# A graph attention layer in float32: Strassen's block products for the weights, and (A h) W for A (h W)

## The chip, the core and the metric

The kernel runs on one core of a Trainium2 chip. The core has a matmul engine (TensorE, PE in the profile; PEld is its weight load), three engines for elementwise work (VectorE: DVE, ScalarE: ACT, GpSimd: POOL), and SyncE (SP), which here only issues transfers between the chip's memory and the core's. TensorE reads operands from SBUF and writes to PSUM, which has eight banks of 512 float32 values in each of 128 partitions. Each engine works through its own list of instructions in order, and semaphores tie the lists together. The metric is the device time of one execution in microseconds (us).

## The reference

The input x has 128 batches of 64 nodes with 512 features, one adjacency matrix serves all batches, and everything is float32:

```
h   = relu(layernorm(x))
Wh  = h W[head]                       # four heads, 512 -> 512
e   = leaky_relu(f1[n] + f2[m], 0.01) # f1, f2: Wh times the halves of a
A   = softmax(e where adj > 0 else -1e9)
h1  = elu(concat over heads of A Wh)  # 2048 features
Wh2 = h1 W_out                        # 2048 -> 512, one head, the same attention
o   = elu(A2 Wh2)
y   = relu(o w1 + b1) w2 + b2 + o
out = x + layernorm(y) * gamma + beta
```

The weights are ten matrices of 512 x 512: four of W, four of W_out, w1 and w2. The product of a tile of 128 tokens with all of them is 10 x 16 matmuls of 128 x 128 with 128 x 512.

## The kernel before

Two batches share a tile of 128 tokens, which gives 64 tiles; inside a tile the attention matrix is block-diagonal, with zeros between the two batches. All weights lie in SBUF from the start on (wh, wo, w1s, w2s). The main loop takes a tile through stages that are staggered over three tiles, so that the vector work of one lies under the matmuls of another:

- `norm1` (L91 to L97): mean and variance on VectorE (L83, L85), the power -0.5 on GpSimd (L89), relu with scale and bias on ScalarE (hn).
- `transpose_h`, `project1`: four transposes, f1 and f2 of all heads (pf, L238) and then, for each head, h W in four matmuls of 512 columns (pm, L244), which ScalarE copies out (L248).
- `softmax` on VectorE and ScalarE; the scores come from one matmul (pe, L182).
- `attend1`: A (h W), transposed: for each head four matmuls of 128 columns (pa, L258), then elu (L227 to L229).
- `project2`: 16 matmuls of 512 columns (pm, L276), and f of the second layer from the result (jf, L284).
- `attend2`, `transpose_out`, and after every fourth tile `feed_forward` on the group of four (L314, L322) with the last layer norm (L326 to L329) and the store.

SyncE issues the loads of x and of adj and the stores of the output; the weights and rows were loaded on ScalarE's queue, the rows of a_heads on GpSimd's. The tile framework sets the order: each engine's list comes from a scheduler that plans the whole program with its own estimates of time, so instructions of different stages interleave in the list, and buffers that are reused bring waits.

A float32 matmul is two instructions on TensorE in the profile (2048 rows for the 1024 matmuls of L244); a transpose is one.

Of the kernel before, what the change touches and what calls it, by code (L numbers as in the profile page):

```python
# [15 lines left out]
NEG = 1.0e9  # L16
# [4 lines left out]
def gat_preln_kernel(  # L21
# [16 lines left out]
    """x + GAT(relu(LN(x))): two batches of 64 nodes share one tile of 128 tokens; attention inside  # L38
    a tile is block-diagonal. Feed-forward runs on groups of G tiles. Everything is float32."""
# [9 lines left out]
    OC = O // P  # L49
    FC = FO // P  # L50
    DC = DF // P
    NT = B * N // P
    G = 4

# [9 lines left out]
    def row_bcast(dst, src):  # L64
        """A row of DRAM into all partitions."""
        nc.scalar.dma_start(out=dst, in_=src[None, :].to_broadcast([P, src.shape[0]]))

# [1 line left out]
    X, HN, HT = {}, {}, {}  # L69

    def load(t):
        X[t] = xp.tile([P, F], FP, tag="x", name=f"x{t}")
        nc.sync.dma_start(out=X[t], in_=xf[ts(t, P), :])
# [5 lines left out]

    def norm_stats(src, tag, t):  # L80
        """mean and (var + eps)^-0.5 per token."""
# [10 lines left out]
    def norm1(t):  # L92
        mean, rstd = norm_stats(X[t], "n1", t)
        nb = sm.tile([P, 1], FP, tag="n1nb", name=f"n1nb{t}")
        nc.vector.scalar_tensor_tensor(nb, mean, -1.0, rstd, ALU.mult, ALU.mult)
        HN[t] = wk.tile([P, F], FP, tag="hn", name=f"hn{t}")
        nc.scalar.activation(HN[t], X[t], AF.Relu, bias=nb, scale=rstd)  # L97

    def transpose_h(t):
        pt = ps.tile([P, KC, P], FP, tag="tp", name=f"pth{t}")  # L100
        for k in range(KC):
            nc.tensor.transpose(pt[:, k, :], HN[t][:, ts(k, P)], ident)
        HT[t] = wk.tile([P, KC, P], FP, tag="hT", name=f"hT{t}")
        nc.scalar.copy(HT[t], pt)  # L104
        del HN[t]

    load(0)

# [1 line left out]
    wh = const.tile([P, H, KC, O], FP, name="wh")  # L110
    for h in range(H):
        nc.scalar.dma_start(out=wh[:, h], in_=W_heads[h].rearrange("(k p) o -> p k o", p=P))
    load(1)
    load(2)
    norm1(0)

    aj = const.tile([P, N], mybir.dt.int32, name="aj")
    for b in range(NB):
        nc.sync.dma_start(out=aj[ts(b, N), :], in_=adj)
    adjm = const.tile([P, N], FP, name="adjm")  # L120
    nc.vector.tensor_scalar(adjm, aj, 0.0, None, ALU.is_gt)
    negm = const.tile([P, N], FP, name="negm")
    nc.vector.tensor_scalar(negm, adjm, NEG, -NEG, ALU.mult, ALU.add)

    blkones = const.tile([P, NB, N], FP, name="blkones")
    nc.vector.memset(blkones, 0.0)
    for b in range(NB):
        nc.vector.memset(blkones[ts(b, N), b, :], 1.0)
    eye = const.tile([P, N], FP, name="eye")
    nc.vector.tensor_add(eye, ident[:, 0:N], ident[:, N:2 * N])  # L130

    # f1 and f2 of the heads are h @ (W a): wa[k, (c, h)] = sum_o W[h, k, o] a[h, c, o].
    wa = const.tile([P, KC, 2 * H], FP, name="wa")
    for c in range(2):
        for h in range(H):
            ab = wk.tile([P, O], FP, tag="y", name=f"ab{c}_{h}")
            nc.gpsimd.dma_start(
                out=ab, in_=a_heads[h:h + 1, c * O:(c + 1) * O].to_broadcast([P, O])
            )
            for k in range(KC):  # L140
                junk = wk.tile([P, FO], FP, tag="junk", name=f"jk{c}_{h}_{k}", bufs=1)
                nc.vector.scalar_tensor_tensor(  # L142
                    junk, wh[:, h, k, :], 1.0, ab, ALU.mult, ALU.mult,
                    accum_out=wa[:, k, c * H + h:c * H + h + 1],
                )

    wo = const.tile([P, H * OC, FO], FP, name="wo")
    for h in range(H):
        nc.scalar.dma_start(
            out=wo[:, ts(h, OC), :],  # L150
            in_=W_out[h * O:(h + 1) * O, :].rearrange("(c p) o -> p c o", p=P),
        )
    ao = const.tile([P, 2, FO], FP, name="ao")
    for c in range(2):
        row_bcast(ao[:, c, :], a_out[c * FO:(c + 1) * FO])
    w1s = const.tile([P, FC, DF], FP, name="w1s")
    nc.scalar.dma_start(out=w1s, in_=w1.rearrange("(k p) d -> p k d", p=P))
    b1s = const.tile([P, DC], FP, name="b1s")
    for d in range(DC):
        nc.scalar.dma_start(out=b1s[:, d:d + 1], in_=b1[ts(d, P)][:, None])  # L160
    w2s = const.tile([P, DC, FO], FP, name="w2s")
    nc.scalar.dma_start(out=w2s, in_=w2.rearrange("(k p) d -> p k d", p=P))
    b2s = const.tile([P, FO], FP, name="b2s")
    row_bcast(b2s, b2)
# [169 lines left out]
    for i in range(NT + 2):  # L334
        if i + 3 < NT:
            load(i + 3)
# [49 lines left out]
```

## Time and profile before

| | |
|---|---|
| median of 3 runs | 2804.86 us (2804.45 to 2805.07) |
| span of the profiled execution, first to last instruction | 2802.2 us |
| its own time around the span, taken as the median less the span | 2.7 us |
| PE busy | 2708.3 us, 97% |
| DVE, ACT, POOL busy | 1185.1, 567.8, 263.5 us |
| moved by DMA | 48.98 MB, mean 17 GB/s |
| granted TensorE clock | 0.997 of full speed |

In the rows of groups a line reads: line of the code, engine, operation, tile written <- tiles read, shape, count, then busy time, mean duration of one in ns, and the idle time of the engine in front of them with what ended it. Rows of the timeline begin with the start and the duration in us. Matmuls are pipelined and their ends are modelled, so the time that one takes of PE is the distance between two starts, not its duration. The rows of windows give, for each stretch, its length and then the busy time with the count in brackets for PE, PEld, DVE, ACT and POOL, the granted clock, the DMA engines' busy share and GB/s.

### The profile page before, as it was taken

Reading aid. Unit: us, or ns where it says so; the run is one execution under the profiler, and the core shown is the slowest. Engines: PE = TensorE matmul, PEld = TensorE weight load, DVE = VectorE, ACT = ScalarE, POOL = GpSimd, SP = SyncE. Lnnn points to the kernel's source line nnn. Section 1 sums busy time; section 2 is a strip of 40 time slices with the busy share of each in tenths; the row PEclk is TensorE's granted clock in tenths of the full one; section 3 lists DMA queues with packets and bytes.
Section 4 is the critical chain, followed back from the end, with each engine's and each line's share of the span. In section 5 each row is a group of like instructions: output and inputs, shape, how many; then the busy total and the mean of one; then the engine's idle time right before and its main releaser. Section 6 shows DMA issues by size and latency. Waiting matters only on the chain.

```text
span 2802.2 us, 23483 instructions
## 1 busy us (share of the span) xinstructions
PE 2708.3 (97%) x8896; PEld 1407.5 (50%) x8896; DVE 1185.1 (42%) x3206; ACT 567.8 (20%) x1025; POOL 263.5 (9%) x271
## 2 busy tenths in 40 slices
PE   3999999999999999999999999999999999999997
PEld 1555555545455454554555555454554545545553
DVE  5344435444254443444444344443544435434433
ACT  1221221212212121121212212122121211212121
POOL 2001001010010101001011010100101000010000
PEclk9999999999999999999999999999999999999998
DMA  6000000000000000000000000000000000000000
GB/s 233 1 0 27 4 1 30 1 31 0 0 31 1 31 1 8 23 1 30 1 23 8 1 31 0 30 1 0 31 1 30 0 1 31 0 27 1 10 6 15
DMA packets 25920, 48.98 MB, mean 17 GB/s; under 512 B 3152, under 2 KB 3152, under 8 KB 25808
## 3 DMA queue, kind: packets, MB, share of 16 engines
q1 hardware_dynamic: 18592, 33.60, 3.6%
q10 hardware_dynamic: 6576, 11.80, 1.2%
q0 software_dynamic: 640, 2.10, 0.2%
q8 instruction: 69, 1.13, 0.2%
q14 instruction: 43, 0.35, 0.0%
HBM read 30.71 MB, written 16.78 MB: 17 GB/s over the span
## 4 chain that ended last, share of the span: by engine, by line
PE 86%; DVE 7%; ACT 2%; POOL 2%; issue 2%; DMA 1%; SPq 0%; POOLq 0%; DVEq 0%; ACTq 0%
PE pm L276 31%; PE pm L244 30%; PE pa L258 8%; PE pf L314 8%; PE pf L322 2%; PE pa L292 2%; POOL n2rs L89 2%; PE pf L238 1%; DVE y L326 1%; ACT wh L280 1%; DVE n2st L83 1%; PE s1pe L182 1%; DVE jf L284 1%; ACT outT L303 1%; DMA ab<-in_L_gnn_a_heads_dram 1%
## 5 line engine op out<-in xcount | busy, mean ns | idle before, releaser
L244 PE MATMUL pm<-wh,hT 128*128 128x512 f32 x2048 | 924.0, 598 | 0.3 <-ACT hT L104 0.3
L276 PE MATMUL pm<-wo,h1T 128*128 128x512 f32 x2048 | 900.1, 592 | 0.0
L276 PEld LDWEIGHTS pm<-wo,h1T 128*128 128x128 f32 x2048 | 384.1, 190 | 476.6 <-issue 476.6
L244 PEld LDWEIGHTS pm<-wh,hT 128*128 128x128 f32 x2048 | 378.6, 190 | 399.2 <-issue 392.1
L284 DVE SCALAR_TENSOR_TENSOR jf<-pm,ao 128x512 f32<-128x512 f32 x128 | 88.5, 691 | 757.4 <-ACT wh L280 755.3
L227 ACT ACTIVATE ex<-pa 128x512 f32<-128x512 f32 x320 | 190.7, 596 | 538.4 <-PE pa L258 458.4
L248 ACT COPY wh<-pm 128x512 f32<-128x512 f32 x256 | 150.0, 586 | 636.1 <-PE pm L244 629.8
L258 PEld LDWEIGHTS pa<-s1AT,wh 128*128 128x128 f32 x2048 | 244.2, 192 | 54.2 <-issue 27.1
L304 POOL TENSOR_TENSOR o<-o,b2s 128x512 f32<-128x512 f32 x64 | 81.5, 1273 | 1977.7 <-PE pto L302 1977.7
L258 PE MATMUL pa<-s1AT,wh 128*128 128x128 f32 x2048 | 254.1, 277 | 10.1 <-DVE s1AT L221 9.3
L314 PE MATMUL pf<-outT,w1s 128*128 128x512 f32 x512 | 230.1, 603 | 5.0 <-ACT outT L303 5.0
L322 PE MATMUL pf<-w2s,rT 128*128 128x512 f32 x512 | 222.3, 592 | 0.0
L228 DVE TENSOR_SCALAR ex<-ex 128x512 f32<-128x512 f32 x320 | 133.2, 420 | 201.0 <-ACT ex L227 200.0
L280 ACT COPY wh<-pm 128x512 f32<-128x512 f32 x64 | 37.5, 586 | 784.9 <-PE pm L276 784.9
L229 DVE SCALAR_TENSOR_TENSOR h1T<-pa,ex 128x512 f32<-128x512 f32 x256 | 173.9, 684 | 5.6
L322 PEld LDWEIGHTS pf<-w2s,rT 128*128 128x128 f32 x512 | 97.3, 190 | 122.5 <-issue 118.6
L314 PEld LDWEIGHTS pf<-outT,w1s 128*128 128x128 f32 x512 | 95.9, 192 | 118.3 <-issue 109.3
L221 DVE COPY s2AT<-s2pt 128x128 f32<-128x128 f32 x64 | 18.6, 291 | 286.2 <-PE s2pt L219 286.1
L326 DVE TENSOR_TENSOR y<-pf,o 128x512 f32<-128x512 f32 x64 | 43.6, 681 | 213.1 <-PE pf L322 213.1
L89 POOL TENSOR_TENSOR n2rs<-n2ve,mhalf 128x1 f32<-128x1 f32 x64 | 60.8, 951 | 394.6 <-DVE n2ve L87 394.6
L238 PE MATMUL pf<-wa,hT 128*128 128x8 f32 x512 | 62.7, 248 | 30.8 <-DVE jk L142 30.3
L305 POOL TENSOR_TENSOR x<-x,bs 128x512 f32<-128x512 f32 x64 | 81.5, 1273 | 21.1 <-ACT hn L97 17.9
(73 smaller groups left out, 1604.3 us busy)
## 6 DMA issues: line engine op xcount, KB each, us to landing
x<-in_x_dram SPq DMA_DIRECT2D x64, 256.0 KB, 2.7
out_dram<-y SPq DMA_DIRECT2D x64, 256.0 KB, 2.0
wh<-in_L_gnn_W_heads_dram ACTq DMA_DIRECT2D x4, 1024.0 KB, 9.7
wo<-in_L_gnn_W_out_dram ACTq DMA_DIRECT2D x4, 1024.0 KB, 15.6
ab<-in_L_gnn_a_heads_dram POOLq DMA_DIRECT2D x8, 256.0 KB, 5.8
w1s<-in_L_gnn_w_dram ACTq DMA_DIRECT2D x1, 1024.0 KB, 13.6
w2s<-in_L_gnn_w_dram ACTq DMA_DIRECT2D x1, 1024.0 KB, 7.6
ao<-in_L_gnn_a_out_dram ACTq DMA_DIRECT2D x2, 256.0 KB, 14.2
```

Of the source, the lines that this page charges most:

```text
L89: nc.gpsimd.tensor_tensor(rstd, ve, mhalf, ALU.pow)
L227: nc.scalar.activation(ex, src, AF.Exp)
L228: nc.vector.tensor_scalar(ex, ex, 1.0, -1.0, ALU.min, ALU.add)
L229: nc.vector.scalar_tensor_tensor(dst, src, 0.0, ex, ALU.max, ALU.add)
L238: nc.tensor.matmul(pf, hT[:, k, :], wa[:, k, :], start=(k == 0), stop=(k == KC - 1))
L244: nc.tensor.matmul(pm, hT[:, k, :], wh[:, h, k, :], start=(k == 0), stop=(k == KC - 1))
L248: nc.scalar.copy(WH1[t, h], pm)
L258: nc.tensor.matmul(pa[:, c, :], w[:, ts(c, P)], AT[:, h, :], start=True, stop=True)
L276: nc.tensor.matmul(pm, hT[:, c, :], wo[:, i, :], start=(i == 0), stop=(i == H * OC - 1))
L284: nc.vector.scalar_tensor_tensor(junk, pm, 1.0, ao[:, c, :], ALU.mult, ALU.mult, accum_out=f[:, c:c + 1])
L314: nc.tensor.matmul(pm, w1s[:, k, ts(d, P)], oT[:, k, :], start=(k == 0), stop=(k == FC - 1))
L322: nc.tensor.matmul(pm, rT[:, d, ts(j, P)], w2s[:, d, :], start=(d == 0), stop=(d == DC - 1))
```

## The change

The kernel is written anew around groups of four tiles (512 tokens), 16 of them. Three things change in what is computed.

**Products in seven block products.** A group's activations are cut into four blocks of 256 tokens by 256 features, a weight matrix into four blocks of 256 x 256, and the product is formed by Strassen's scheme in the variant of Winograd: seven products of 256 x 256 blocks instead of eight. The sums of weight blocks are made once at the start (`prepare`, on GpSimd) and stored in the chip's memory (tc); the sums of activations are made by GpSimd for layers 1 and 2 (`sums`, `each`) and by VectorE for the feed-forward (`blocks`). The results are combined partly in PSUM (p2, p7, p3 and p4 add into the bank of an earlier product) and partly by VectorE (t, s15, and the last sums).

**Weights streamed.** No weight matrix stays in SBUF. `piece` loads the 256 x 256 block or sum that a product needs, 256 KB, on SyncE's queue into a ring of 12 buffers: 70 pieces for a group, 1120 in all. 480 of them come from the weights themselves in rows of 1 KB, 640 from the stored sums in rows of 2 KB. x is loaded into two buffers and loaded again for the residual (xr).

**(A h) W in layer 1.** The attention is applied to h, in front of W. For each tile, half of the features and batch, two matmuls of 256 columns (all four heads) read 64 partitions, the first batch on the upper half of PE's rows and the second on the lower half, into two PSUM banks (L403). ScalarE and VectorE each copy one of them out (L413, L415). The elu becomes two passes on ScalarE and one on VectorE (L423 to L425).

The order of a group in the program: `project1` for four heads, `attend1` of the next group, `feed_forward` of the group before, `project2`; norms and softmaxes (`stage_a`, two groups ahead) and the second attention (`stage_e`) are given out in pieces between the products (`side`). The last product of a unit (`late`) runs after the first two of the next one.

```diff
-    xp = ctx.enter_context(tc.tile_pool(name="xp", bufs=9))
+    ring = ctx.enter_context(tc.tile_pool(name="ring", bufs=12))
+    big = ctx.enter_context(tc.tile_pool(name="big", bufs=1))
...
-    ps = ctx.enter_context(tc.tile_pool(name="ps", bufs=2, space=bass.MemoryType.PSUM))
+    dram = ctx.enter_context(tc.tile_pool(name="dram", bufs=1, space=bass.MemoryType.DRAM))
+    ps = ctx.enter_context(tc.tile_pool(name="ps", bufs=6, space=bass.MemoryType.PSUM))
...
+    def prepare(m):
+        w = big.tile([P, KC, O], FP, tag=("h11", "h12")[m % 2], name=f"pw{m}")
+        nc.scalar.dma_start(out=w, in_=mats[m].rearrange("(k p) o -> p k o", p=P))
...
+        s = big.tile([P, 4, 2, Q], FP, tag=("h22", "hS")[m % 2], name=f"pt{m}")
+        nc.gpsimd.tensor_tensor(s[:, 0], b12, b11, ALU.subtract)
+        nc.gpsimd.tensor_tensor(s[:, 2], b22, b12, ALU.subtract)
+        nc.gpsimd.tensor_tensor(s[:, 1], b22, s[:, 0], ALU.subtract)
+        nc.gpsimd.tensor_tensor(s[:, 3], b21, s[:, 1], ALU.subtract)
+        TC[m] = dram.tile([P, 4, 2, Q], FP, name=f"tc{m}")
+        nc.sync.dma_start(out=TC[m], in_=s)
+
+    def piece(m, p):
+        w = ring.tile([P, 2, Q], FP, tag="w", name=f"w{m}_{p}")
...
+        nc.sync.dma_start(out=w, in_=src)
+        return w
...
+        def p1():
+            gb[1] = bank(f"g1_{name}")
+            product(1, gb[1], True)
+            gb["s1"] = wk.tile([P, 2, T], FP, tag="s1", name=f"s1_{name}")
+            nc.scalar.copy(gb["s1"], gb[1])
+
+        def p6():
+            gb[6] = bank(f"g6_{name}")
+            product(6, gb[6], True)
+            gb["t"] = wk.tile([P, 2, T], FP, tag="t", name=f"t_{name}")
+            nc.vector.tensor_tensor(gb["t"], gb[6], gb["s1"], ALU.add)
+            post("t", gb["t"])
...
+        def p7():
+            product(7, gb[6], False)
+            post("c22", gb[6], gb["s15"])
...
+        return [p1, p6, p5, p2, p7, p3, p4]
...
+            for o in range(2):
+                for k in range(2):
+                    nc.tensor.matmul(
+                        bk[:, o, :], w[:, k, ts(o, P)], a[:, k, :],
+                        start=first and o == 0 and k == 0, stop=k == 1, skip_group_check=True,
+                    )
...
+    def sums(s1, a11, a12, a22, s2, s3, s4):
+        nc.gpsimd.tensor_tensor(s2, s1, a11, ALU.subtract)
+        nc.gpsimd.tensor_tensor(s4, a12, s2, ALU.subtract)
+        nc.gpsimd.tensor_tensor(s3, a22, s2, ALU.subtract)
...
+                for c in range(2):
+                    for b in range(NB):
+                        rows = slice(b * N, (b + 1) * N)
+                        nc.tensor.matmul(
+                            banks[b][:, c, :].rearrange("p (h n) -> p h n", h=H),
+                            src[rows, off + c * P:off + (c + 1) * P],
+                            at[rows, :, rows], start=True, stop=True, skip_group_check=True,
+                        )
...
+            s1, a22 = tt[1][:, 0:2], tt[1][:, 2:4]
+            nc.vector.tensor_tensor(s1, s1, a22, ALU.add)
+            nc.vector.tensor_tensor(s2, s1, a11, ALU.subtract)
...
+    for g in range(NG):
+        if g >= 1:
+            side.extend(stage_e(g - 1))
+        for h in range(H):
+            project1(g, h)
+        flush_side()
+        flush_late()
+        if g + 1 < NG:
+            attend1(g + 1)
+        if g >= 1:
+            feed_forward(g - 1)
+            flush_late()
+        side.extend(stage_a(g + 2))
+        project2(g)
+        flush_side()
```

How the lists move, at three places. First TensorE, where a tile's layer 1 stood and where (A h) of the next group now follows the last products of a head (before, then the change; pm and pa are products and attention, g a product's bank, w a piece, z and zs blocks of (A h) and their sums, pz a bank of (A h), at the attention, hn the tile):

```order
L244 MATMUL pm_7_0_1577<-wh,hT_1486 128x512 x2
L258 MATMUL pa_2_1550<-s1AT_1528,wh_6_2_1428 128x128 x4
L258 MATMUL pa_3_1560<-s1AT_1528,wh_6_3_1435 128x128 x4
L182 MATMUL s1pe_1586<-s1dg_1584,blkones 128x256
L244 MATMUL pm_7_1_1605<-wh,hT_1486 128x512 x4
```
```order
L229 MATMUL g_a_3_2843<-zs_z_3_2777,w_3_2873 128x256 x4
L229 MATMUL g_a_3_2822<-z_2_1846,w_4_2884 128x256 x4
L403 MATMUL pz_12_0_2900<-at_2469,hn_2265 128x256
L403 MATMUL pz_12_1_2901<-at_2469,hn_2265 128x256
L403 MATMUL pz_12_0_2900<-at_2469,hn_2265 128x256
L403 MATMUL pz_12_1_2901<-at_2469,hn_2265 128x256
```

The attention's short matmuls between the products are gone; a block product is one row of four matmuls of 256 columns, and (A h) stands as a phase of its own in which the two batches alternate.

Second VectorE: before, at the end of a group, among the last layer norms (y, n2); in the change at the end of (A h) and the start of the feed-forward (x, n1 are the first norm; ot the transposed output o; zs_o its sums). The semaphores that a row waits for stand behind it:

```order
L83 BN_STATS n1st_2549<-x_2170 128x6 [waits DMAHW7_49]
L326 TENSOR_TENSOR y_2139<-pf_6_2134,o_1820 128x512 [waits DMAHW6_49,PE_49]
L85 BN_AGGR n1mv_2551<-n1st_2549 128x2 [waits DVE_49]
L83 BN_STATS n2st_2141<-y_2139 128x6 [waits DVE_49]
L87 TENSOR_SCALAR n1ve_2553<-n1mv_2551 128x1 [waits DVE_49]
```
```order
L262 BN_STATS n1st_4361<-x_3443 128x6 [waits DMAHW3_49]
L415 COPY z_3_2899<-pz_15_1_2957 128x2x4x64 [waits PE_49]
L264 BN_AGGR n1mv_4363<-n1st_4361 128x2 [waits DVE_49]
L266 TENSOR_SCALAR n1ve_4365<-n1mv_4363 128x1 [waits DVE_49]
L276 SCALAR_TENSOR_TENSOR n1nb_4369<-n1mv_4363,n1rs_4367 128x1 [waits Activation_49,Pool_49]
L555 TENSOR_TENSOR ot_1_2965<-ot_1_2965 128x512 [waits Activation_49]
L262 BN_STATS n1st_4373<-x_3445 128x6 [waits DMAHW4_49]
L556 TENSOR_TENSOR zs_o_2996<-ot_1_2965,ot_1_2964 128x512 [waits DVE_49]
```

All four norms of a later group have moved into this phase, and L555 and L556, which make operands of the feed-forward's products, stand behind the loads of x.

Third SyncE, before in the middle of the program, in the change between the feed-forward's and layer 2's pieces (w a piece, tc a stored sum):

```order
L73 DMA x_6420<-in_x_dram 128x512 [waits DMAHW7_49,Pool_49]
L330 DMA out_dram<-y_6371 128x512 [waits DMAHW0_49,DVE_49]
L73 DMA x_6609<-in_x_dram 128x512 [waits DMAHW1_49,Pool_49]
L330 DMA out_dram<-y_6389 128x512 [waits DMAHW2_49,DVE_49]
L73 DMA x_6797<-in_x_dram 128x512 [waits DMAHW3_49,Pool_49]
```
```order
L151 DMA w_7_3113<-tc_445 128x512 [waits DMAHW0_49,PE_49]
L92 DMA x_3332<-in_x_dram 128x512 [waits DMAHW1_49,Activation_49]
L92 DMA x_3334<-in_x_dram 128x512 [waits DMAHW2_49,Activation_49]
L92 DMA x_3443<-in_x_dram 128x512 [waits DMAHW3_49,DMAHW1_49,Activation_49]
L92 DMA x_3445<-in_x_dram 128x512 [waits DMAHW4_49,DMAHW2_49,Activation_49]
L151 DMA w_3_3121<-in_L_gnn_w_dram 128x2x256 [waits DMAHW5_49,PE_49]
```

Loads of x and stores that had a queue to themselves now stand among the weight pieces.

More of the change, by code (lines that the diff above doesn't have):

```diff
@@ new lines, in gat_preln_kernel @@
+    blkones = const.tile([P, NB, N], FP, name="blkones")
+    nc.vector.memset(blkones, 0.0)
+    for b in range(NB):
+        nc.vector.memset(blkones[ts(b, N), b, :], 1.0)
+    eye = const.tile([P, N], FP, name="eye")
+    nc.vector.tensor_add(eye, ident[:, 0:N], ident[:, N:2 * N])
+    mats = [W_heads[h] for h in range(H)]
+    mats += [W_out[h * O:(h + 1) * O, :] for h in range(H)]
+    mats += [w1, w2]
+    M1, M2 = H * 2, H * 2 + 1
+    TC = {}
+    wa = const.tile([P, KC, 2 * H], FP, name="wa")
```

572 lines of the change are left out of this document (362 added, 210 removed).

## The prediction

> **What bounds the kernel now.** I read the page's busy times first, then the chain that ended last, then a steady stretch by windows, then single stretches of the timeline.
>
> ```profile
> PE 2708.3 (97%) x8896; PEld 1407.5 (50%) x8896; DVE 1185.1 (42%) x3206; ACT 567.8 (20%) x1025; POOL 263.5 (9%) x271
> PE 86%; DVE 7%; ACT 2%; POOL 2%; issue 2%; DMA 1%; SPq 0%; POOLq 0%; DVEq 0%; ACTq 0%
> ...
> 1457.32 0.99 POOL L89 TENSOR_TENSOR n2rs<-n2ve,mhalf 128x1 f32<-128x1 f32 x1 [17.11 <-DVE n2ve L87]
> 1627.92 0.99 POOL L89 TENSOR_TENSOR n2rs<-n2ve,mhalf 128x1 f32<-128x1 f32 x1 [17.11 <-DVE n2ve L87]
> 1457.30:1627.90 170.60, 168.70 (x557) 87.73 (x556) 72.28 (x197) 35.40 (x64) 16.07 (x16) 1.00 0.04 13
> ...
> 50.07 2.91 PE L244 MATMUL pm<-wh,hT 128*128 128x512 f32 x3
> ```
>
> The same norm of two successive groups of four tiles stands 170.60 us apart, and the window over one such period has PE busy for 168.70 of it, DVE for 72.28, POOL for 16.07 (its columns are PE, PEld, DVE, ACT, POOL). The kernel is TensorE's matmul stream. So I split the profiled span of 2802.2 us into a start of 50.1 (the first weight product), 16 periods of 170.6 (2729.6) and a rest of 22.5 at the end. The median of the runs is 2.7 above the span; I add that at the end.
>
> What a matmul instruction takes of PE is read from start to start, since the printed durations overlap:
>
> ```profile
> 1400.50 0.60 PE L302 MATMUL pto<-ident,o 128*128 128x128 f32 x4
> 1400.93 0.60 PE L102 MATMUL pth<-ident,hn 128*128 128x128 f32 x4
> ...
> 1404.72 2.00 PE L258 MATMUL pa<-s1AT,wh 128*128 128x128 f32 x16
> 1406.56 0.96 PE L238 MATMUL pf<-wa,hT 128*128 128x8 f32 x8
> 1407.37 0.68 PE L244 MATMUL pm<-wh,hT 128*128 128x512 f32 x1
> ...
> 1410.96 0.60 PE L182 MATMUL s1pe<-s1dg,blkones 128*128 128x256 f32 x2
> 1411.39 10.46 PE L244 MATMUL pm<-wh,hT 128*128 128x512 f32 x24
> 1421.69 0.27 PE L219 MATMUL s2pt<-ident,s2A 128*128 128x128 f32 x1
> ```
>
> A float32 matmul is two such instructions (2048 rows for 1024 matmuls at L244); a transpose is one. 512 columns: 10.30/24 = 0.429 us each. 256 columns: 0.43/2 = 0.215. 128 columns: 1.84/16 = 0.115. 8 columns: 0.81/8 = 0.10, which is then the weight load. A transpose: 0.43/4 = 0.107. At 256 columns the loads still hide: 0.215 is half of 0.429.
>
> **The change part by part. (1) Products.** Per group of four tiles before: 4 x 40 matmuls of 512 columns, 320 x 0.429 = 137.3 us. Now: 70 steps (7 per head in layer 1, 4 x 7 in layer 2, 14 in the feed-forward) of four matmuls of 256 columns, 560 x 0.215 = 120.4, or 1.72 a step. Attention's 16 matmuls a tile (128 x 0.115 = 14.7) go; (A h) takes eight a tile of 256 columns and half the rows. What stays: the second attention 8 x 0.429, 52 transposes x 0.107, 32 x 0.10 for f, 8 x 0.215 and 2 x 0.215 for the score products: 14.4. Before, this adds to 166.8 with 0.9 for the narrow score products, so some 4 of the 170.6 were waiting. Each product's first reader, a VectorE add (0.69) or a ScalarE copy (0.59), has two to three steps, 3.4 to 5.2 us, before PE writes the same bank again; that covers it, and without the cover it would be 0.8 us for each of ten units. Where PE no longer is the last one to be waited for is the phase of (2).
>
> **(2) The side phase.** In front of each feed-forward stands (A h) of the next group. Two batches use two halves of PE's rows; no row shows whether these run at once. Bounds: one after the other, 64 x 0.215 = 13.8; fully at once, 6.9. But the order puts more into this phase. On VectorE, where the old order had one norm among the last layer norms, four first norms now stand among the evacuations, and the feed-forward's first sums stand behind them (the rows of VectorE's order in the section on the change): L555 and L556 (lines of the changed kernel) make the operands of the feed-forward's second product, and both stand behind loads of x. On SyncE, where only x and out alternated, each x now waits for ScalarE to free one of two buffers, and the weight pieces of the feed-forward's last steps and of layer 2's first queue behind it (SyncE's rows there). Who waits for them is PE, in the steps that those pieces serve. Prices (group rows: busy, mean ns; the last row: KB and us to landing):
>
> ```profile
> L248 ACT COPY wh<-pm 128x512 f32<-128x512 f32 x256 | 150.0, 586 | 636.1 <-PE pm L244 629.8
> L97 ACT ACTIVATE hn<-x,n1nb,n1rs 128x512 f32<-128x512 f32 x64 | 53.1, 831 | 0.2 <-DVE n1nb L95 0.2
> L229 DVE SCALAR_TENSOR_TENSOR h1T<-pa,ex 128x512 f32<-128x512 f32 x256 | 173.9, 684 | 5.6
> L83 DVE BATCH_NORM_STATS2 n1st<-x 128x6 f32<-128x512 f32 x64 | 43.9, 685 | 7.9 <-DMA x<-in_x_dram 7.9
> L304 POOL TENSOR_TENSOR o<-o,b2s 128x512 f32<-128x512 f32 x64 | 81.5, 1273 | 1977.7 <-PE pto L302 1977.7
> L89 POOL TENSOR_TENSOR n1rs<-n1ve,mhalf 128x1 f32<-128x1 f32 x64 | 35.9, 561 | 116.3 <-ACT hn L97 67.7 <-DVE n1ve L87 48.5
> x<-in_x_dram SPq DMA_DIRECT2D x64, 256.0 KB, 2.7
> ```
>
> From the phase's start: ScalarE does an elu pass, a copy, the other pass and a copy, then the first hn (4 x 0.59 + waits + 0.83: 4.0) and frees its x; load 2.7 (6.8); statistics and their two small followers (7.8), POOL's power (8.6), the bias (9.3), hn 0.83 (10.2), which frees x for the third tile; load (13.0), statistics and one copy (15); its bias waits for POOL, which has two sums o+b2s (2.5) and a small one in front of the power (16.5); then L555, a statistic and L556, 0.69 each: 18.6. PE could have been there after 6.9 to 13.8 plus 4.5 of transposes and first product that (1) counts. I take 18.6, so 14.1 above (1); bounds 7 and 17.
>
> **(3) Waits inside the products.** At the start of layer 1 VectorE has, from the last product's sum to the attention weights, some 17 operations of 512 (0.69, one of 1024 at an estimated 1.2): 12.3 us, where PE has 10.7 to do: 1.6. In the feed-forward the last block's add, relu and two sums cost 1.5. With the 4 of before: 7 a group; bounds 4 and 14, since VectorE is busy for some 45 of the 58 us of layer 1.
>
> **(4) GpSimd.** It goes from 8 large sums a group to 36 (36 x 1.27 = 46), and 40 more for the weights at the start. What that does to VectorE:
>
> ```profile
> 1403.05 1.27 POOL L305 TENSOR_TENSOR x<-x,bs 128x512 f32<-128x512 f32 x1 [0.60 <-ACT hn L97]
> 1403.27 1.12 DVE L175 TENSOR_TENSOR s2dg<-eye,f 128x64 f32<-128x64 f32 x1
> ...
> 1438.68 0.22 DVE L175 TENSOR_TENSOR s2dg<-eye,f 128x64 f32<-128x64 f32 x1
> ```
>
> The same operation took 1.12 beside POOL's sum, ending with it, and 0.22 alone. Its inputs both lie in SBUF. So such VectorE work waits for up to 1.27 a time; the start is costed with it, in the periods it is in the upper bounds.
>
> **(5) Weight stream.** 1120 pieces of 256 KB instead of resident weights:
>
> ```profile
> q1 hardware_dynamic: 18592, 33.60, 3.6%
> 20.00:40.00 20.00, 0.00 (x0) 0.00 (x0) 13.10 (x39) 0.00 (x0) 3.36 (x6) 1.00 1.05 384
> ```
>
> The row gives packets, MB and the share of 16 engines. 3.6% of their span over 18592 packets is 87 ns for at most 2 KB: a piece with 128 rows of 2 KB takes 128 x 87/16 = 0.70 us, one of the three in seven with 256 rows of 1 KB 0.70 (by bytes) to 1.39 (by rows). A step of PE takes 1.72, and the ring holds 12 pieces, 20.6 us, against the 14 us that SyncE stands at the x loads in (2). The stores of y stand in the same queue, one product step into layer 2: they wait for the layer norms of four tiles (by the rows above some 12 to 15 us after the last feed-forward product), also under 20.6. So nothing is added; what it costs without that cover is a rival.
>
> **(6) Start and end.**
>
> ```profile
> L142 DVE SCALAR_TENSOR_TENSOR jk<-wh,ab 128x512 f32<-128x512 f32 x32 | 23.0, 719 | 10.6 <-DMA ab<-in_L_gnn_a_heads_dram 6.6 <-issue 2.5 <-DVE jk L142 0.7
> 11.47 0.68 DVE L142 SCALAR_TENSOR_TENSOR jk<-wh,ab 128x512 f32<-128x512 f32 x1
> 2764.26 16.78 PE L314 MATMUL pf<-outT,w1s 128*128 128x512 f32 x32 [0.68 <-ACT outT L303]
> 2750.00:2803.00 53.00, 36.62 (x81) 15.75 (x79) 17.47 (x42) 5.26 (x9) 6.22 (x6) 0.82 0.05 20
> ```
>
> From 11.5 on, each of four heads has 8 x 0.72 on VectorE and 4 x 1.27 on POOL, both with two SBUF inputs, so one after the other: 10.9 x 4, to 55. Two softmaxes of two tiles follow (9.5 each, and seven waits of half a POOL sum: 14 each) while POOL prepares six more matrices: 83; transposes, (A h), the first sums: 95. PE did 9 of a period's work there: 86 counts. Bounds 71 and 101. At the end the scores, second attention and layer norms of the last group stand alone: about 20 + 3 + 8, and 3 for the lower clock that such gaps bring (0.82 in the last window; 32 matmuls took 16.78 instead of 13.7): 34; bounds 25 and 40.
>
> **Sum.** 86 + 16 x (120.4 + 14.4 + 7) = 2268.8, + 14 phases x 14.1 + one of 7 = 204.4, + 34: 2593 of span, with 2.7 around it 2596. Lower bounds together: 71 + 16 x 138.8 + 15 x 7 + 25 = 2422; upper: 101 + 16 x 148.8 + 15 x 17 + 40 = 2777.
>
> **Rivals.** (a) *The phase of (2) is short*: the loads and norms arrive early and PE packs it. Then 86 + 16 x 138.8 + 15 x 7 + 34 = 2446, with 2.7: 2449. It needs the two halves of (A h) to run at once; one after the other the phase is at least 13.8 longer, about what the forecast has. For it: the order places loads early; against: the chain needs two turns of the x buffers whatever PE does. The Trainium skill (TensorE: Matmul & The Clock Gate, Part 3: Packing small matmuls) says that matmuls on different row groups run at once, some four ns apart; no run shows it yet, and by it (a) stays open, without it (a) falls out and the forecast stands. (b) *POOL and VectorE block each other*: half a POOL sum for each of 36 is 23 us of VectorE a group; in layer 1 and in (2) some 8.5 reach PE: 2596 + 15 x 8.5 = 2724. For it the 1.12 row; against, most adds have one input in PSUM. (c) *The weight stream is late*, and the kernel slower: SyncE serves in order, so a wait there beyond 20.6 us reaches PE one for one, and pieces that cost over 1.72 us pace it. 14 us a group, that is a stand of 35 us or 1.92 us a piece on average (1 KB rows at 222 ns, 2.5 times the row above), is the point where the gain is gone; one piece at a time, at the 2.7 of the x load, gives 70 x 2.7 = 189 a group, some 3150. Against it: 384 GB/s in the window above, a piece in 0.68. The Trainium skill (DMA: Bandwidth & Descriptors, Anatomy of one DMA) gives a fixed part of 2.0 us and bytes at 436 GB/s, an estimate of 2.6 us a piece; the 2.7 agrees, and by that alone the change would be slower, if pieces did not overlap. (d) That the change doesn't do what it says: the built program has 4480 products of 256 columns for 2560 of 512; excluded.
>
> **How the numbers follow.** Forecast 0.67, (a) 0.14, (b) 0.13, (c) 0.05, anything else 0.01. Predicted 2596. Range 2455 to 2725: from (a) to (b), with (c) and the ends of the bounds outside. What a measurement here can tell from no change is about 0.2%, 6 us. Faster 0.94, same 0.01, slower 0.05.
>
> **What would show it.** Right: PE's product steps 1.72 apart; a period near 156; first product near 95; in the phase before the feed-forward PE idle, released by VectorE's L556. Wrong: PE waiting for pieces (releaser DMA), which is (c); a (A h) phase that ends in the products with no idle, (a); VectorE operations at 1.2 or more throughout layer 1 with PE released by them, (b).

## The result and the profile after

The changed kernel takes 2623.07 us (2622.25 to 2624.64), against 2804.80 in the runs beside it: 0.9354 of the time before, 95% interval 0.9341 to 0.9367. The forecast was 2596, in a range of 2455 to 2725. The profiled execution has a span of 2621.4 us.

The page's busy times and chain of waits:

```profile
PE 2398.3 (91%) x11552; PEld 2021.8 (77%) x11552; DVE 1467.3 (56%) x2630; ACT 744.1 (28%) x1345; POOL 1018.5 (39%) x887
PE 72%; DVE 12%; POOL 7%; ACT 3%; issue 3%; DMA 3%; SPq 0%; DVEq 0%; POOLq 0%; ACTq 0%
```

PE lost 310 us of work, and the kernel only 182: PE's share falls from 97% to 91%, and 14 points of the chain go from PE to the other engines, DMA and "issue" (time in which an engine waits for nothing that the profile shows). The windows say where. The first row covers ten whole periods, the others one period by its stages: layer 1, (A h), the transposes of o, the feed-forward's first product, the rest of its first unit, its second unit, and the start and rest of layer 2.

```profile
549.87:2116.83 1566.96, 1489.10 (x7223) 1259.25 (x7222) 878.52 (x1601) 461.25 (x840) 597.81 (x520) 0.98 0.46 138
...
1331.96:1391.38 59.42, 58.45 (x278) 48.31 (x276) 41.90 (x75) 28.55 (x52) 12.01 (x9) 1.00 0.43 121
1391.38:1401.89 10.51, 8.07 (x65) 6.38 (x65) 7.18 (x15) 7.45 (x14) 2.55 (x3) 1.00 0.33 91
1401.89:1407.30 5.41, 2.86 (x18) 2.62 (x18) 3.56 (x9) 2.63 (x5) 3.99 (x5) 0.80 0.32 97
1407.30:1411.13 3.83, 3.81 (x17) 2.77 (x16) 3.55 (x6) 1.66 (x3) 3.23 (x3) 0.84 0.05 4
1411.13:1421.16 10.03, 10.03 (x47) 8.85 (x47) 4.18 (x9) 2.54 (x6) 0.55 (x1) 1.00 0.47 137
1421.16:1437.56 16.40, 14.31 (x68) 12.21 (x66) 9.15 (x15) 2.09 (x5) 12.93 (x12) 0.95 0.43 125
1437.56:1445.31 7.75, 7.75 (x33) 6.68 (x32) 5.84 (x12) 0.00 (x0) 5.83 (x5) 0.89 0.35 108
1445.31:1488.94 43.63, 43.63 (x207) 38.14 (x206) 12.38 (x25) 1.17 (x2) 18.71 (x16) 1.00 0.62 198
```

A period is 156.7 us (forecast 155.9). Layer 1 and most of layer 2 run as one stream of matmuls at full clock. What is lost lies in the 46 us between them, and it is lost twice: PE is idle there, and behind each longer idle stretch the clock is lower. The waits of PE (what waited <- for what: us in all, times, longest; those that stand at the program's start are left out):

```profile
PE g_d L243 <- DVE o L591: 29.5, 14, 2.3
PE pto L546 <- ACT ot L547: 29.3, 16, 2.6
PE pzS L403 <- DVE z L415: 24.8, 14, 1.9
...
PE g_c L229 <- DVE zs_o L556: 8.5, 6, 2.9
```

Here pz and pzS are banks of (A h), pto holds the transposes of o, g_c and g_d are the feed-forward's two units. None of PE's waits in the whole run is for a weight piece. The timeline of the phase that the forecast called the side phase (PE, then VectorE, then ScalarE):

```profile
1399.07 0.91 PE L403 MATMUL pzS<-at,hns 64*128 64x256 f32 x5 [1.81 <-DVE z L415]
1405.54 1.97 PE L546 MATMUL pto<-ident,o 128*128 128x128 f32 x8 [2.55 <-ACT ot L547]
1411.13 1.99 PE L229 MATMUL g_c<-zs_o,w 128*128 128x256 f32 x8
...
1397.73 0.69 DVE L262 BATCH_NORM_STATS2 n1st<-x 128x6 f32<-128x512 f32 x1 [1.96 <-DMA x<-in_x_dram]
1398.34 0.67 DVE L415 COPY z<-pz 128x512 f32<-128x512 f32 x1
1407.58 1.21 DVE L276 SCALAR_TENSOR_TENSOR n1nb<-n1mv,n1rs 128x1 f32<-128x1 f32 x1 [1.40 <-POOL n1rs L268]
1409.92 1.15 DVE L556 TENSOR_TENSOR zs_o<-ot,ot 128x512 f32<-128x512 f32 x1
...
1404.20 0.81 ACT L278 ACTIVATE hn<-x,n1nb,n1rs 128x512 f32<-128x512 f32 x1 [2.03 <-DVE n1nb L276]
1404.92 1.05 ACT L547 COPY ot<-pto 128x512 f32<-128x512 f32 x2
```

VectorE waits 1.96 us for x with an evacuation of (A h) queued behind; ScalarE waits 2.03 for a bias with the copies of o queued behind. L556 ends at 1411.07, and PE starts the product that reads it at 1411.13. So the phase lasts 19.75 us from its first matmul (1391.38). The same trace holds a control: in the last phase of this kind, in front of the last feed-forward but two, there is no further group to normalise.

```profile
2333.93 3.72 PE L403 MATMUL pz<-at,hn 64*128 64x256 f32 x32
...
2341.43 1.09 PE L546 MATMUL pto<-ident,o 128*128 128x128 f32 x8
...
2346.97 1.99 PE L229 MATMUL g_c<-zs_o,w 128*128 128x256 f32 x8 [1.34 <-DVE zs_o L556]
```

There the 64 instructions of (A h) take 7.50 us, 0.117 each, which is half of 0.215: two batches on two halves of the rows do run at once. The phase lasts 13.04, so a later group's norms, with their loads of x, cost 6.7 us a group. There are 13 phases with such norms and this one without.

### The profile page after: what moved, and what is told of

It is laid out like the page before. It is cut to its first block, busy times and chain, and to the rows that moved or that the text cites. A ratio compares the mean times of both kernels' runs of the same rounds, so it can differ in the third digit from the quotient of the medians.

```text
span 2621.4 us, 32503 instructions
## 1 busy us (share of the span) xinstructions
PE 2398.3 (91%) x11552; PEld 2021.8 (77%) x11552; DVE 1467.3 (56%) x2630; ACT 744.1 (28%) x1345; POOL 1018.5 (39%) x887
## 4 chain that ended last, share of the span: by engine, by line
PE 72%; DVE 12%; POOL 7%; ACT 3%; issue 3%; DMA 3%; SPq 0%; DVEq 0%; POOLq 0%; ACTq 0%
PE g_b L243 30%; PE g_a L229 22%; PE g_c L229 7%; PE g_d L243 3%; PE pa L528 2%; POOL o L586 2%; DMA x<-in_x_dram 2%; PE pf L299 2%; POOL zs_z L251 1%; DVE jk L129 1%; PE s1pe L317 1%; PE s1pt L365 1%; ACT hn L278 1%; PE pto L546 1%; PE pth L292 1%
## 5 line engine op out<-in xcount | busy, mean ns | idle before, releaser
L243 PE MATMUL g_b<-w,h 128*128 128x256 f32 x2560 | 573.0, 384 | 0.0
L243 PEld LDWEIGHTS g_b<-w,h 128*128 128x128 f32 x2560 | 493.8, 194 | 70.0 <-ACT z L413 0.5
L229 PE MATMUL g_a<-z,w 128*128 128x256 f32 x1536 | 369.7, 380 | 0.0
L229 PE MATMUL g_a<-zs_z,w 128*128 128x256 f32 x1536 | 364.4, 381 | 4.9 <-POOL zs_z L251 4.9
L229 PEld LDWEIGHTS g_a<-zs_z,w 128*128 128x128 f32 x1536 | 289.7, 190 | 60.7 <-issue 19.1
L229 PEld LDWEIGHTS g_a<-z,w 128*128 128x128 f32 x1536 | 288.5, 190 | 45.6 <-issue 9.1
L243 PE MATMUL g_b<-w,hS 128*128 128x256 f32 x1024 | 226.2, 379 | 0.0
L243 PEld LDWEIGHTS g_b<-w,hS 128*128 128x128 f32 x1024 | 194.6, 190 | 26.9 <-issue 0.5
L243 PE MATMUL g_d<-w,rt 128*128 128x256 f32 x512 | 134.2, 409 | 31.6 <-DVE o L591 29.5
L424 ACT ACTIVATE exc<-exc 128x512 f32<-128x512 f32 x256 | 156.3, 627 | 4.0
L586 POOL TENSOR_TENSOR o<-s_d,o 128x256 f32<-128x256 f32 x64 | 59.2, 945 | 181.8 <-ACT s_d L187 181.3
L403 PE MATMUL pz<-at,hn 64*128 64x256 f32 x768 | 113.3, 394 | 11.4 <-DVE zS L415 8.2
```

What stands on the lines that cost most here:

```text
L229: nc.tensor.matmul(bk[:, o, :], w[:, k, ts(o, P)], a[:, k, :], start=first and o == 0 and k == 0, stop=k == 1, skip_group_check=True,)
L243: nc.tensor.matmul(bk[:, j, :], a[:, k, ts(j, P)], w[:, k, :], start=first and i == 0 and k == 0 and j == 0, stop=i == len(ms) - 1 and k = ...
L403: nc.tensor.matmul(banks[b][:, c, :].rearrange("p (h n) -> p h n", h=H), src[rows, off + c * P:off + (c + 1) * P], at[rows, :, rows], star ...
L424: nc.scalar.activation(ex, ex, AF.Exp, scale=-1.0)
L586: nc.gpsimd.tensor_tensor(o, a[:, j], o, ALU.add)
```

## The experiments

Times are medians. The first six of these kernels differ from the changed kernel (2623.1) by the edit shown alone. The phase is the stretch from the first (A h) matmul to the feed-forward's second product, 19.75 us in the changed kernel.

**Four buffers for x.**

```diff
-        X[t] = wk.tile([P, F], FP, tag="x", name=f"x{t}")
+        X[t] = wk.tile([P, F], FP, tag="x", name=f"x{t}", bufs=4)
...
-    ring = ctx.enter_context(tc.tile_pool(name="ring", bufs=12))
+    ring = ctx.enter_context(tc.tile_pool(name="ring", bufs=11))
```

> Four buffers for x instead of two (and 11 ring slots for weight pieces instead of 12, for the room). Theory of the prediction (x load, first norm and its followers hold the phase in front of the feed-forward): the 1.8 us before the zS products and the 2.6 us before the pto transposes shrink, 3 to 4 us in each of 15 phases, so 2560 to 2580 us. Rival (the phase is held by its 32 evacuations, 16 on ScalarE and 16 on VectorE, and by first norms that wait for hn, not for x): the phase stays at 19.8 us and the time at 2612 to 2625.

2599.97 us (ratio 0.928, 0.9261 to 0.9300): 23 us less, between the two. The waits ahead of the (A h) products and of pto shrink (from 36 to 24 us in all and from 29.3 to 6.6), but a new one stands at the end of the same chain. The last row covers ten periods:

```profile
PE g_c L229 <- DVE zs_o L556: 39.8, 16, 2.9
...
1398.59 1.23 DVE L276 SCALAR_TENSOR_TENSOR n1nb<-n1mv,n1rs 128x1 f32<-128x1 f32 x1 [2.04 <-POOL n1rs L268]
1399.74 1.83 DVE L555 TENSOR_TENSOR ot<-ot 128x512 f32<-128x512 f32 x1
1396.79 1.26 POOL L549 TENSOR_TENSOR o<-o,b2s 128x512 f32<-128x512 f32 x1
1398.02 0.54 POOL L268 TENSOR_TENSOR n1rs<-n1ve,mhalf 128x1 f32<-128x1 f32 x1
1398.53 2.48 POOL L549 TENSOR_TENSOR o<-o,b2s 128x512 f32<-128x512 f32 x2
...
549.30:2096.85 1547.55, 1470.77 (x7223) 1240.94 (x7222) 880.12 (x1601) 460.21 (x840) 596.90 (x520) 0.99 0.47 140
```

x is no longer late; now the power n1rs stands behind o+b2s on GpSimd, and L555 takes 1.83 instead of 0.68, and ends 0.56 after GpSimd's next two sums do. The phase is 18.5 us in this period. But PE's idle time has only moved: 7.7 us a period against 7.8. What falls is PE's busy time for the same matmuls, 147.1 us a period against 148.9, and that is the clock (see the half-tile additions below): the stall in the feed-forward's second unit, which this edit does not touch, is still 2.1 to 2.3 us, but the clock no longer drops behind it. So the 23 us are no measure of what the loads of x cost.

**o+b2s on VectorE.**

```diff
-            nc.gpsimd.tensor_tensor(OUT[g, j], OUT[g, j], b2s, ALU.add)
+            nc.vector.tensor_tensor(OUT[g, j], OUT[g, j], b2s, ALU.add)
```

> The sum o+b2s (four a group, 1.27 us each on GpSimd) goes to VectorE, nothing else. Theory (in the phase in front of the feed-forward these sums stand ahead of the norms' power on GpSimd, 0.8 us, and hold VectorE's small L276 at 1.21 instead of 0.16 and its L556 at 1.15 instead of 0.68): 2.3 us less in 15 phases, less what four sums of 0.7 on VectorE put in front of L556: 2590 to 2612. Rival (the x loads alone hold the phase): 2616 to 2630.

2583.83 us (0.9214, 0.9200 to 0.9227): 39 less, the theory's way and 6 below its range. PE's wait at pto falls from 29.3 to 13.3 us. Over ten periods PE's idle time falls by 1.3 us a period and its busy time for the same work by 0.9, so that some 40% of the gain is clock.

**The feed-forward's half-tile additions on VectorE.**

```diff
-                    nc.gpsimd.tensor_tensor(o, a[:, j], o, ALU.add)
+                    nc.vector.tensor_tensor(o, a[:, j], o, ALU.add)
```

> The eight additions of half tiles in the feed-forward's second product go from GpSimd to VectorE. Theory (PE's 2.1 us in front of the last step there is VectorE's add standing behind GpSimd's sums, with layer 1's next sums in front of those): the 2.1 go in 15 phases, so 2590 (2583 to 2600). Rival (VectorE is the shorter resource there, and eight more operations of about 0.4 us push its adds back): 2615 to 2640.

2573.94 us (0.9175, 0.9162 to 0.9189): 49 less, half as much again as the waiting time that was removed, and 9 below the theory's range. The second unit falls from 16.2 us to 13.2. In the changed kernel the list of GpSimd there reads as follows (then VectorE's and PE's rows that wait for it):

```profile
1429.16 1.27 POOL L253 TENSOR_TENSOR zs_z<-z,zs_z 128x512 f32<-128x512 f32 x1
1430.39 1.26 POOL L251 TENSOR_TENSOR zs_z<-zS,z 128x512 f32<-128x512 f32 x1
1431.61 1.41 POOL L586 TENSOR_TENSOR o<-t_d,o 128x256 f32<-128x256 f32 x2
1432.97 1.40 POOL L586 TENSOR_TENSOR o<-s_d,o 128x256 f32<-128x256 f32 x2
...
1433.73 0.42 DVE L591 TENSOR_TENSOR o<-g_d,o 128x256 f32<-128x256 f32 x1 [3.59 <-POOL o L586]
...
1434.89 2.88 PE L243 MATMUL g_d<-w,rt 128*128 128x256 f32 x8 [2.09 <-DVE o L591]
```

Sums for the next layer 1, which have some 50 us of time, stand ahead of additions for which PE waits: VectorE's L591 comes after L586 on the same o, and only its reading frees the PSUM bank. The surplus over the 2.1 us is clock: behind this stall TensorE runs at half speed for a while, into the start of layer 2. (Over ten periods idle time makes 2.5 of the 3.0 us gained and clock only 0.6, because the first unit, whose stalls stay, now loses more of it.) In the record of the granted clock of the changed kernel every change falls on one grid with steps of 3.41 us. Here are the grid steps around both stalls, the one at pto and this one (PE's busy time is the second number, PEclk the third from the right):

```profile
1401.72:1405.13 3.41, 1.26 (x10) 0.86 (x8) 2.71 (x6) 1.38 (x3) 1.97 (x4) 1.00 0.28 77
1405.13:1408.54 3.41, 3.00 (x11) 2.77 (x12) 1.97 (x5) 2.01 (x4) 3.41 (x4) 0.50 0.22 77
...
1432.44:1435.85 3.41, 1.32 (x6) 0.87 (x5) 1.86 (x5) 0.00 (x0) 3.41 (x5) 1.00 0.44 139
1435.85:1439.26 3.41, 3.41 (x9) 2.70 (x8) 2.29 (x8) 0.00 (x0) 1.32 (x2) 0.50 0.09 25
```

In a step PE is idle for 2.15 and 2.09 us, and the next step of 3.41 us has exactly half the clock.

**(A h) on all rows.** Each product reads all 128 rows and the whole block matrix, so that its zeros take the other batch out; the two batches can no longer share PE.

```diff
-                            src[rows, off + c * P:off + (c + 1) * P],
-                            at[rows, :, rows], start=True, stop=True, skip_group_check=True,
+                            src[:, off + c * P:off + (c + 1) * P],
+                            at[:, :, rows], start=True, stop=True, skip_group_check=True,
```

> (A h) with both batches' rows in each product (128 rows, the other batch's weights being the zeros of the block matrix), so the 64 products of a phase cannot share PE: 13.8 us of PE instead of 6.9. If the phase is held by x loads and evacuations, as predicted, the extra PE time lies beside those waits and the time stays within 2615 to 2635. If PE itself is what the phase is short of, it grows by 3.3 (13.8 less the 10.5 that the products' part of the phase takes now) to 6.9 in 16 phases: 2674 to 2731.

2652.19 us (0.9453, 0.9439 to 0.9467): 29 more, between the two.

```profile
1407.75 7.07 PE L403 MATMUL pz<-at,hn 128*128 128x256 f32 x32
```

Now they are 0.216 apart (32 in 6.91, to the start of the next), 13.8 us for 64 instead of 7.5 unhindered. Of these 6.3 us a group only 1.8 (29 / 16) reach the end. But the theory's reason, waits that stood there anyway, holds for the smaller part: over ten periods PE's idle time falls from 7.8 to 6.4 us a period. Its busy time grows by 3.4 where 6.3 were added, and the missing 2.9 are clock, whose mean rises from 0.972 to 0.989.

**Four slots for weight pieces.** `bufs=12` of the ring becomes `bufs=4`.

> Four slots for weight pieces instead of twelve: a cover of 6.9 us instead of 20.6. If a piece costs the queue 0.7 to 1.4 us and lands 3.3 us after its issue, as read, four slots suffice between the phases, and only the stand of SyncE behind the x loads (10 to 14 us) reaches PE, 0 to 5 us in 15 phases: 2621 to 2700. If landing to landing is what counts (rival c: pieces hardly overlap), PE is paced by pieces all over, at 2 us or more a step instead of 1.72: 2850 and up.

2706.04 us (0.9645, 0.9631 to 0.9660): 83 more, 6 above the theory's range. Waits of PE, and SyncE's list in one period:

```profile
PE g_b L243 <- DMA w<-tc: 66.1, 32, 4.1
...
1324.68 0.44 SPq L151 DMA_DIRECT2D w<-tc  x1
1331.25 0.34 SPq L604 DMA_DIRECT2D out_dram<-o  x1
```

The stand that reaches PE is not that at the x loads, as expected, but the one at the stores of y (1324.7 to 1331.3). Elsewhere four slots nearly keep up (PE waits another 6.1 us in all for pieces of the feed-forward's second product), so pieces overlap.

**Ordinary products in the feed-forward.** Its two units do eight quarter products each, with no sums of activations and no half-tile additions; layers 1 and 2 keep the seven products. The helper `plain` is not shown.

```diff
-        run_unit(unit(f"c{g}", product_t(M1, lambda p: bl1[p]), post1))
+        run_unit(plain(f"c{g}", product_t(M1, lambda p: bl1[p]), post1))
...
-        run_unit(unit(f"d{g}", product_n([M2], lambda p, i: bl2[p]), post2))
+        run_unit(plain(f"d{g}", product_n([M2], lambda p, i: bl2[p]), post2))
```

> The feed-forward's two products go by the ordinary eight quarter products each, without Strassen's sums (layer 1 and 2 keep theirs). Theory (Strassen's two saved steps there, 2 x 1.72 a group, are given back by what its sums cost: PE's 2.1 us in front of the last step, some 1.4 of lower clock after it, and GpSimd's additions): within 15 us of the changed kernel, 2606 to 2636. Rival (each saved step counts in full): 2621 + 16 x 3.45, 2660 to 2680.

2570.58 us (0.9165, 0.9152 to 0.9179): 52 less. Both expectations fall: in the changed kernel Strassen's scheme in the feed-forward is a loss, though PE has 256 instructions more without it. Each unit takes 13.8 us, at full clock and with no wait, where seven products took 14.1 and 16.2. Ten periods:

```profile
542.04:2077.32 1535.28, 1495.11 (x7383) 1271.53 (x7381) 742.06 (x1451) 447.11 (x820) 532.98 (x460) 0.99 0.49 144
```

PE's idle time falls by 3.8 us a period, and the 16 further instructions (3.4 us) nearly take that up; the period is 3.2 shorter because the clock is higher (mean 0.989 against 0.972). So most of the loss is not the sums' time itself but the half clock that the stalls around them bring.

**Three edits together:** four x buffers, o+b2s and the half-tile additions on VectorE.

> Three edits together: four x buffers (11 ring slots), the feed-forward's half-tile additions and o+b2s on VectorE. If x loads and GpSimd's sums are two links of one chain, the chain falls only with both: with four x buffers what is left in the phase is 1.5 us of queue on GpSimd, 1.1 at L276 and 1.1 at L555, so 2600 - 47 (the additions, measured) - 15 x 3.7: 2500 to 2525. Rival (the gains are the same waits of PE, paid once): 2545 to 2575.

2511.84 us (0.8955, 0.8941 to 0.8968), as expected. The single edits gave 23, 39 and 49, 111 in sum; together they give 111. That the sum is met is partly chance: nearly all of the first gain, 40% of the second and a fifth of the third are clock, which depends on where the stalls fall. Ten periods:

```profile
535.61:2025.87 1490.26, 1457.02 (x7222) 1233.92 (x7221) 896.01 (x1701) 460.23 (x840) 492.87 (x420) 1.00 0.49 145
```

Against the changed kernel's ten periods PE runs the same work (7222 rows of matmuls, 7223 before) in 145.7 us a period instead of 148.9: 3.2 less from clock alone. Its idle time falls from 7.8 to 3.3; the single edits removed 0.1 (x), 1.3 and 2.5, 3.9 in sum. So the four x buffers, worth 0.1 of idle time alone, are worth some 0.7 with the other two, which is what two links of one chain would do. Of the 7.7 us gained, 42% is clock. This is the fastest version found.

**The three edits with ordinary products in the feed-forward.**

> The kernel with the three edits (2511.8), with the feed-forward by ordinary quarter products. Theory (Strassen's two saved steps in the feed-forward count once its operands are no longer late): the feed-forward's two units go from 26.9 to 27.6 us and 1.8 of transposes that stood between them go to layer 2: 2.6 a group and 3.5 in the last, 2550 to 2560. Rival (Strassen costs more than it saves there whatever stands ahead of it, as it did without the edits, by 52): 2460 to 2505.

2546.07 us (0.9079, 0.9063 to 0.9094): 34 more than with Strassen's products, 4 less than the theory's range. So the scheme's two saved steps are worth 34 us of the 55 that they count (16 x 2 x 1.72) once their operands come in time, and minus 52 when they do not.

**(A h) in layer 2.** The three edits, and attend1 of the next group is given out between layer 2's products, in the two small PSUM buffers.

```diff
-                banks = [bank(f"pz{nm}_{t}_{b}") for b in range(NB)]
+                banks = [aux([P, 2, T], f"pz{nm}_{t}_{b}") for b in range(NB)]
...
-        if g + 1 < NG:
-            attend1(g + 1)
         if g >= 1:
             feed_forward(g - 1)
             flush_late()
+        if g + 1 < NG:
+            for j in range(G):
+                side.append(lambda j=j: attend1(g + 1, [j]))
         side.extend(stage_a(g + 2))
```

> As the kernel with the three edits, and (A h) of the next group is no phase of its own: its tiles run as side work between the products of layer 2, through the two small PSUM buffers. Theory (the phase is bound by 32 evacuations and the first norms, which layer 2 can cover, since PE has 50 us of products there): PE's period comes near its own work, 120.9 + 14.4 + 6.9 and 2 to 4 us of waits, 145: 2420 to 2460. Rival (two PSUM buffers make each pair of products wait for its evacuation inside layer 2): no better than the three edits alone.

2635.65 us (0.9391, 0.9376 to 0.9407): 124 more than the edits alone: the rival held, and the theory's range was missed by some 175. A wait of PE at the start of layer 1, and layer 1 by windows:

```profile
1336.71 0.66 PE L292 MATMUL pth<-ident,hn 128*128 128x128 f32 x4 [1.70 <-DVE z L416]
...
1330.69:1338.00 7.31, 5.57 (x32) 4.00 (x31) 5.93 (x11) 3.04 (x5) 5.48 (x4) 1.00 0.25 75
1338.00:1345.35 7.35, 7.35 (x22) 5.54 (x22) 3.88 (x6) 0.58 (x1) 5.24 (x6) 0.54 0.16 39
1345.35:1401.40 56.05, 55.40 (x266) 45.84 (x265) 39.04 (x66) 28.01 (x51) 10.96 (x9) 1.00 0.42 119
```

(A h) now ends in the first products of layer 1, whose sums and whose softmaxes it feeds; the stall stands there, and some 7 us at about half the clock behind it. Layer 1 with the transposes takes 70.7 us. The pairs of products cost more when scattered (eight of them took 1.06 to 2.06 us, 0.94 where they are packed). How much of the loss is the PSUM buffers and how much the place was not separated.

**Eight buffers for hn.** The additions and o+b2s on VectorE as before, x in two buffers, hn in eight, the ring at seven.

> Eight buffers for hn (four for its sums), two for x, seven ring slots, the half-tile additions and o+b2s on VectorE. Theory (with spare hn buffers the first norms need not wait for (A h), so the phase falls to its evacuations, 9.8 to 11 us instead of 12.2): 2470 to 2500. Rival (two x buffers put the load back into the chain, as before the edits): 2525 to 2560.

2551.18 us (0.9094, 0.9078 to 0.9109): the rival's range. Waits of PE for pzS <- VectorE's z are 23.9 us again (24.8 in the changed kernel): with two buffers of x the load is back in the chain. The ring of seven adds 5.9 us of waits for pieces in the whole run, so hn alone was not separated.

**The heads' weight sums on VectorE,** with the three edits: `prepare` uses VectorE for m < 4.

> The kernel with the three edits (2511.8), with the four sums for each of the four heads' weights at the start on VectorE instead of GpSimd. Theory (GpSimd's sums and VectorE's operations with two SBUF inputs run one after the other, so a sum costs VectorE 1.27 there and 0.69 when it does it itself): 16 x 0.6 less, 2496 to 2506. Rival (they run at once but for chance, and VectorE, the longer one, only gets more to do): 16 x 0.69 more, 2518 to 2526.

2513.99 us (0.8965, 0.8952 to 0.8979), 2 us more than without, which the intervals (0.8941 to 0.8968 there) do not tell from nothing: neither. VectorE's 32 products for f (jk) fall from 1138 ns each to 749, so they did stand behind GpSimd's sums. But that is 12 us, and the 16 sums at 0.68 take back 11.

## Why the prediction was right, and where it was not

**(1) Steps.** Right: 1.73 apart in layers 1 and 2 (forecast 1.72), with 0.97 us of PE idle in the 59.4 of layer 1. What the step count left out is that fourteen of the seventy, those of the feed-forward, did not pay: their 14 x 1.72 = 24 us stand in the trace as 30.3 with 1.9 of transposes and f in them.

**(2) The side phase.** 18.6 us forecast, 19.75 measured, by the chain that was named: x buffer, load, statistics, GpSimd's power behind o+b2s, bias, hn, L555, L556. Its links are shown by the phase with no norms (13.04) and by where PE's waits go: with x on time they move from pzS and pto to L556, behind o+b2s (39.8 us), and with o+b2s gone from GpSimd too the wait at L556 falls to 2.6 us in all (the three edits). The times of the single edits are no measure of a link, since clock is mixed into them. The sign that was named is only half right: L556 releases the product, but PE's idle time stands earlier, at pzS and pto, since the same late norms also stand in front of evacuations on VectorE and ScalarE; at L556 itself PE waits 8.5 us in all.

**(3) Waits in the products.** This step failed in its cause. The 1.5 us put down to the feed-forward's last add, relu and sums did not occur; 2.1 stood at the end of the second unit instead, behind the order of GpSimd's list, where the forecast had read VectorE's and SyncE's. And the clock in the periods was left out: two stalls, each with 3.4 us at half clock behind it, are 3.2 us a period, half of it in the phase of (2). Outside that phase 0.97, 2.1 and 1.6 make 4.7 of the 7 that were put there. That the period came within 0.8 us of the forecast is therefore partly luck: without the 3.2 of clock, which the forecast did not have, it would be 153.5, 2.4 below it.

**(4) GpSimd and VectorE.** "Up to 1.27 a time" is too small. At the start, VectorE first:

```profile
16.62 4.46 DVE L129 SCALAR_TENSOR_TENSOR jk<-pw,ab 128x512 f32<-128x512 f32 x1
...
16.82 1.27 POOL L136 TENSOR_TENSOR pt<-pw 128x512 f32<-128x512 f32 x1
18.04 1.26 POOL L137 TENSOR_TENSOR pt<-pw 128x512 f32<-128x512 f32 x1
19.26 1.26 POOL L138 TENSOR_TENSOR pt<-pw,pt 128x512 f32<-128x512 f32 x1
```

One VectorE operation of 0.68 waited through three sums, until GpSimd's list had a gap, though its record begins 0.2 us before theirs. The Trainium skill (SBUF — State Buffer, SBUF: two separate sides) says that such an operation and one of GpSimd hold a port pair in turn, each for its whole instruction; the trace agrees, and adds that sums which follow each other without a gap are not parted. Rival (b) priced this at 8.5 us a group, in layer 1 and in (2) together. In layer 1 PE waits 0.97 in all, so there it costs next to nothing; in the phase of (2) it is a link of the chain, and all four sums o+b2s, with their place in GpSimd's list, are worth 39 / 15 = 2.6 a group, some 40% of it clock.

**(5) Weight stream.** Right: no wait in the changed kernel. The ring of twelve is what makes it so; with four the price is 83 us. The section of the Trainium skill from which the forecast had 2.6 us a piece (DMA: Bandwidth & Descriptors, Anatomy of one DMA) describes transfers that GpSimd issues; here SyncE issues them. The pieces landed 2.9 to 3.9 us after their issue (medians), and one every 1.73 us kept up, so they do overlap.

**(6) Start and end.** First product at 97.4 (forecast 95). But the first group's layer 1 takes 74.5 us, and those from the third group on some 59.4:

```profile
97.42:171.88 74.46, 60.35 (x287) 50.24 (x285) 44.68 (x73) 27.11 (x46) 24.06 (x22) 0.91 0.40 122
```

The second group's norms and softmaxes run in it, with 14 us of PE idle, and part of it is at half clock (0.91). The forecast counted them as ordinary side work: 15 us missed.

The difference of 28 us in the span (2593 to 2621.4) is then: 2 for the first product, 15 for that first layer 1, 11 for the twelve full periods from 393.1 on (156.8 each), and by subtraction some 10 in the rest of the first group and at the end. Against these stand 10 from the two shorter periods in front of and behind the twelve: the second group's, 153.2, and the one with no norms, 148.5, which the forecast counted in full. **Rivals.** (a) fell although its condition, halves at once, was met: the norms held the phase. (c) did not come even with a third of the ring. The chance for "faster" rested on the count of products, and that held.

## What to carry to other kernels

Saving matmuls pays only where their operands are on time: the same two steps a group were worth +34 us or -52, depending on what stood ahead of the sums; most of the 52 was clock lost behind stalls. When an algorithm moves work from TensorE to the engines beside it, read each engine's list for what stands in front of an instruction that PE waits for, GpSimd's too, and move work without urgency (or its engine) before adding buffers. A stall of PE of about 2 us can cost nearly twice its length. And when an edit changes the time, compare PE's idle time and its busy time for the same work before giving the gain to the edited wait: with four x buffers nearly all of it was clock.

## What was not expected of the hardware

Short stalls of PE were enough to halve the granted clock: 2.1 and 2.55 us in the rows above, some 3 and 2 us after their start, for 3.41 us (twice that in two of the ten periods, and twice or three times that with (A h) in layer 2, behind stalls of 1.7). In the three edits' kernel, whose stalls in the periods are all under 1 us, the clock is 1.00.

The price is not the same each time: with four x buffers the feed-forward's first unit, with a stall of 2.2 to 2.9 us in it, took 15.5, 16.2 and 17.9 us in three successive groups. The grid explains it: the last two of these stalls are alike, 2.92 us each. In the second group it falls on two steps (1397.74:1401.16 and 1401.16:1404.57), with PE idle for 1.3 and 1.7 us, and the clock stays at 1.00; in the third group one step (1554.76:1558.17) has 2.0 us, and the next step has 0.50. In the changed kernel's periods every drop came behind a step with 1.7 to 2.6 us of idle time, and no step with more than 1.92 was without one. In other kernels here the bound lies a little elsewhere (1.3 to 1.7 with (A h) in layer 2), so it is a figure of this kernel and not a rule.

The Trainium skill (TensorE: Matmul & The Clock Gate, Part 1: The HAM clock gate) gives two states, half and full clock, and a free-running window of 3.4 us; the 0.50 and the 3.4 us agree with it, and so does the changing price. It puts the drop behind an idle window or more of that length; here some 2 us of idle time within one window sufficed.
